# A Mamba block with a routed expert layer on one core: inputs laid out by partition, eps as a bias, ranking's bank copied by ACT, the first turn moved behind the last row product

## The chip, the cores and the metric

The kernel runs on one core of a Trainium2 chip. The metric is the device time of one execution in microseconds. The program is one launch; the inputs may be laid out anew on the host, but no arithmetic is done there. The engines are called as the profile calls them: PE is TensorE (its matmuls) and PEld its weight loads, DVE is VectorE, ACT is ScalarE, POOL is GpSimd, SP is the engine that only issues DMAs. Each of them works through its own queue in order.

## The reference

The input x has 4096 rows (tokens) of 256 numbers. Everything is fp32.

```python
# Mamba block, D_INNER 512, 16 states
xz = x @ W_in                                   # 256 -> 1024: conv half and gate half
y = causal depthwise conv(conv half, 4 taps) + conv_b
convolved = silu(y)
x_dbl = convolved @ W_x                         # 512 -> 33: delta, B, C
delta = softplus(x_dbl[..., :1])
h[t] = exp(delta * -exp(A_log)) * h[t-1] + delta * B * convolved[..., :16]
ssm = sum(h * C)                                # one number for each token
x = layernorm(x + ((ssm + convolved * D_param) * silu(gate half)) @ W_out)
# expert layer: each token goes to the one expert with the largest logit
expert = argmax(x @ Wr.T + br)                  # 8 experts
out = relu(x @ W1[expert].T + b1[expert]) @ W2[expert].T + b2[expert]
x = layernorm(x + out)                          # (x - mean) / sqrt(var + 1e-5)
```

## The kernel before, in words

**Two parts, overlapped.** The first part goes over the tokens in 8 blocks of 512 (NB = 8, TB = 512). The second part goes over 37 blocks of 128 rows that are sorted by expert (SURE = 37), and two more that run only if the data need them. PE's order is written out by hand: the scheduler is told to leave PE alone (line 109), and lines 808 to 915 are PE's program. The instructions of the other engines are put in order by the scheduler, by its own estimate of when each can run.

**Block k of the first part** is the body of the loop at line 808, and it works on several blocks of tokens at once. `project(k, 0..7)` (line 511) multiplies the block's transposed x (`xTb`) by W_in (`win`), 128 columns at a time: two matmuls of 512 columns (line 526). They are fp32, and the profile counts two records for each. The first four column blocks are evicted by ACT twice (lines 533 and 535), and DVE does the convolution's other three taps on them (line 539). The other four go through silu on ACT (line 531). For the very first product, `project(0, 0)`, the 512 tokens are split into two halves of 256.

For the block before (`a = k - 1`), `gauge` and `gauge_out` (lines 554 and 568) make delta, B and C; they contain the exponential `e` on ACT (line 590) and a chain of tiny DVE steps up to `sr` (line 611). `look` and `look_out` (lines 646 and 661) bring the router's share of x. `scan` (line 615) turns `sr` on PE into the bank `pt` (line 620) and runs the recurrence on DVE; its last step `hC` (line 631) is the last reader of `pt`. For the block before that (`b = k - 2`), `gate` (line 634) makes the product `py` and DVE's `cv`, and `project_out(b, 0..3)` (line 676) multiplies by W_out for 128 rows each (`po`, line 680), adds x and takes the statistics; after the fourth it takes the root (lines 693 to 696) and writes the normalised rows to `x1d` in HBM. `choose` (line 709) finds each row's expert. For `c = k - 3`, `rank` (line 735) counts each row's place within its expert with six small matmuls into one bank `pr`; DVE reads that bank (line 754, `rk`), works out `col` and `row` (line 761), compares them with constants into `colh` (DVE) and `rowh` (line 769: four instructions, on GpSimd for the blocks 0 to 4, on DVE for 5 to 7), and `place` (line 775) multiplies those two into the bank `pz` (line 780).

**PSUM.** The bank tag `tr` has two buffers that all the small products take in turn: `px`, `pxo`, `pr`, `pn`, `prx`, `pf`, `pt`, `pg`, `pz` and `pi`. A product therefore waits until the last but one has been read. When `blocks_of` takes a bank (`pn`, line 279) between `rank` and `look`, as in block 5 and block 7, `prx` (line 653) gets the bank of `pr`.

**The expert blocks** are a generator (`blocks`, line 481) whose quarters are drawn by `expert(n)`: two halves of the hidden layer (`hidden`, line 421: 16 matmuls of 128 columns in each, line 431), then the two halves of the second layer (`close`, line 445, line 452), with `turn(b + 1)` (line 411) ahead of the first of them. `turn` puts a block's gathered rows `xg` through PE into the bank `pg` and copies them (`xgT`). The gathers `xg` and the weights `we` are indirect DMAs from GpSimd (lines 399 and 405); they are issued in `prefetch`. `hidden` evicts its first half on ACT (line 439) and its second on DVE (line 441). `finish` ends with a layernorm of the block (line 238). The list `fill` (line 818) says how many quarters are drawn at each of the eight places of blocks 6 and 7 of the first part. The first turn, `turn(0)`, stands by itself in block 6, behind `scan` (line 862).

**The start.** SP and ACT issue the loads (lines 150 to 158): x's first block in four pieces of 128 KB, W_in in three pieces (the first 128 columns, 384 more, the other 512), and behind the pieces of x on ACT's queue the small `conv_w` and `conv_b`. The other small constants follow on SP's queue. PE does 12 transposes of the identity meanwhile (WARM, line 188).

Of the kernel before, what the change touches and what calls it, by code (L numbers as in the profile page):

```python
# [35 lines left out]
F32 = mybir.dt.float32  # L36
# [9 lines left out]
P = 128  # L46
# [16 lines left out]

WARM = 12

# [23 lines left out]
def mamba_moe(  # L89
# [4 lines left out]
    W_in: bass.AP,  # L94
    conv_w: bass.AP,
    conv_b: bass.AP,
    W_x: bass.AP,
    A_log: bass.AP,
    D_param: bass.AP,
    W_out: bass.AP,  # L100
    W_outT: bass.AP,
    WrT: bass.AP,
    br: bass.AP,
    experts: bass.AP,
# [21 lines left out]
    def load(i):  # L126

        xTb = a2.tile([P, DC, TB], F32, tag="xTb", name=f"xTb{i}")
        at = slice(i * TB, (i + 1) * TB)
        if i:  # L130
            nc.sync.dma_start(xTb, xT[:, at].rearrange("(c p) t -> p c t", p=P))

        xb = a2.tile([P, JT, D + NE], F32, tag="xb", name=f"xb{i}")
        st[i] = {"xTb": xTb, "xb": xb}
# [8 lines left out]

    win = const.tile([P, DC, 2 * DI], F32, name="win")
    first = TB // 2

    def columns(at):
        nc.sync.dma_start(win[:, :, at], W_in[:, at].rearrange("(c p) n -> p c n", p=P))

    for at in (slice(0, first), slice(first, TB)):  # L150
        nc.sync.dma_start(st[0]["xTb"][:, 0, at], xT[0:P, at])
        nc.scalar.dma_start(st[0]["xTb"][:, 1, at], xT[P : 2 * P, at])
        columns(slice(0, P) if at.start == 0 else slice(P, DI))
    cw = const.tile([P, CC, KC], F32, name="cw")
# [10 lines left out]
    al = const.tile([NS, 1], F32, name="al")  # L165
    dp = const.tile([P, CC], F32, name="dp")

    wout = const.tile([P, CC, D + NE], F32, name="wout")
    brb = const.tile([P, NE], F32, name="brb")
    nega = const.tile([NS, 1], F32, name="nega")  # L170

    def load_later():

        nc.sync.dma_start(wx[:, :, 0:XW], W_x.rearrange("(c p) n -> p c n", p=P))
        nc.sync.dma_start(al, A_log)
        nc.sync.dma_start(dp, D_param)
        nc.sync.dma_start(woutT, W_outT.rearrange("(c p) n -> p c n", p=P))
        nc.sync.dma_start(wout[:, :, 0:D], W_out.rearrange("(c p) d -> p c d", p=P))
        nc.sync.dma_start(brb, br.to_broadcast([P, NE]))
# [58 lines left out]
    def layernorm(pool, rows, n, done, name):  # L238
# [272 lines left out]
    def project(i, c):  # L511
# [11 lines left out]

        for at in (slice(0, first), slice(first, TB)) if i == c == 0 else (slice(0, TB),):
            for dc in range(DC):
                nc.tensor.matmul(  # L526
                    pm[:, at], lhsT=win[:, dc, c * P : (c + 1) * P], rhs=xTb[:, dc, at],
                    start=(dc == 0), stop=(dc == DC - 1),
                )
# [116 lines left out]
    def look(i):  # L646
# [3 lines left out]
        for dc in range(DC):  # L650
            for h in range(2):
                g = (2 * dc + h) * Q
                nc.tensor.matmul(
                    prx[g : g + Q, 0:n], lhsT=wr[:, dc, :],
                    rhs=st[i]["xTb"][:, dc, h * n : (h + 1) * n], start=True, stop=True,
                    tile_position=(0, g),
                )
# [18 lines left out]
    def project_out(i, j):  # L676
# [58 lines left out]
    def rank(i):  # L735
# [17 lines left out]
        rk = a2.tile([P, JT, NE], F32, tag="rk", name=f"rk{i}")  # L753
        nc.vector.tensor_tensor(rk, prv.rearrange("p (j e) -> p j e", e=NE), oh, ALU.mult)
        nc.vector.tensor_reduce(best, rk, AX.X, ALU.add)
# [52 lines left out]
    for k in range(NB):  # L808
# [169 lines left out]
```

## Time and profile before

| | us |
|---|---|
| median of 3 runs | 506.21 (505.69 to 506.3) |
| the profiled execution | 507.57 |
| its span in the profile | 505.9 |
| PE busy in the span | 492.2 |
| DVE busy in the span | 344.0 |
| first product of block 0 starts (line 526) | 4.59 |
| its second half starts | 6.21 |
| second column block starts | 7.85 |
| block 6 of the first part, first turn starts (line 415) | 176.63 |
| last matmul ends | 499.28 |

The span is the time from the first to the last instruction of the profiled execution; the time of the runs holds what lies around it as well. In the page, a group of instructions is given by its line, engine and operation, with what it writes and reads (out<-in). "Idle before" is the time in which the engine had nothing to do ahead of that instruction, with the instruction that released it. A matmul's end is modelled, so PE counts as busy also where it runs slower than it could. Names that end in a number are given without it. Stretches of time are counted from the start of the span.

### The profile page before, as it was taken

Reading aid. Unit: us, or ns where it says so; the run is one execution under the profiler, and the core shown is the slowest. Engines: PE = TensorE matmul, PEld = TensorE weight load, DVE = VectorE, ACT = ScalarE, POOL = GpSimd, SP = SyncE. Lnnn points to the kernel's source line nnn. Section 1 sums busy time; section 2 is a strip of 40 time slices with the busy share of each in tenths; the row PEclk is TensorE's granted clock in tenths of the full one; section 3 lists DMA queues with packets and bytes.
Section 4 is the critical chain, followed back from the end, with each engine's and each line's share of the span. In section 5 each row is a group of like instructions: output and inputs, shape, how many; then the busy total and the mean of one; then the engine's idle time right before and its main releaser. Section 6 shows DMA issues by size and latency. Waiting matters only on the chain.

```text
span 505.9 us, 7858 instructions
## 1 busy us (share of the span) xinstructions
PE 492.2 (97%) x2746; PEld 375.4 (74%) x2746; DVE 344.0 (68%) x1090; ACT 223.5 (44%) x472; POOL 181.7 (36%) x189
## 2 busy tenths in 40 slices
PE   7999999999999999999999999999999999999994
PEld 4443545555454576777889999999999999999994
DVE  2587869798999978869799785454545454545443
ACT  3786768778777865844351312212221222122111
POOL 2003011434355444324425234334433443344333
PEclk9998999999999999999999999999999999999998
DMA  7401012120309826407657598999755422811640
GB/s 234 147 1 43 0 43 83 43 84 24 102 1 378 318 63 220 188 0 268 231 198 261 210 361 303 344 349 349 284 202 195 159 105 53 344 58 32 229 182 23
DMA packets 23737, 84.87 MB, mean 168 GB/s; under 512 B 5934, under 2 KB 15665, under 8 KB 20242
## 3 DMA queue, kind: packets, MB, share of 16 engines
q0 software_dynamic: 9360, 69.60, 37.6%
q1 hardware_dynamic: 13378, 14.50, 9.0%
q8 instruction: 22, 0.36, 0.3%
q10 hardware_dynamic: 960, 0.27, 0.3%
q14 instruction: 17, 0.14, 0.1%
HBM read 102.75 MB, written 9.31 MB: 222 GB/s over the span
## 4 chain that ended last, share of the span: by engine, by line
PE 77%; DVE 15%; DMA 3%; ACT 2%; issue 2%; SPq 0%; POOLq 0%; POOL 0%; DVEq 0%; ACTq 0%
PE ph L431 26%; PE pe L452 25%; PE pm L526 11%; PE po L680 8%; DVE acc L539 7%; PE py L638 2%; DVE cv L640 2%; PE pg L415 2%; PE px L561 2%; DMA xg<-x1d,tidx 1%; DMA win<-in_W_in 1%; DVE lg L725 1%; PE pz L780 1%; PE pt L620 1%; DVE h L626 0%
## 5 line engine op out<-in xcount | busy, mean ns | idle before, releaser
L431 PEld LDWEIGHTS ph<-xgT,we 128*128 128x128 f32 x1184 | 138.5, 192 | 4.6 <-issue 1.6
L431 PE MATMUL ph<-xgT,we 128*128 128x128 f32 x1184 | 139.9, 275 | 0.0
L452 PE MATMUL pe<-we,hT 128*128 128x256 f32 x592 | 135.0, 380 | 0.0
L526 PE MATMUL pm<-xTb,win 128*128 128x512 f32 (+1 forms) x260 | 121.6, 598 | 1.2 <-DMA win<-in_W_in 0.7
L452 PEld LDWEIGHTS pe<-we,hT 128*128 128x128 f32 x592 | 109.4, 190 | 14.0 <-DVE best L724 0.8
L539 DVE SCALAR_TENSOR_TENSOR acc<-xc,cw,acc 128x512 f32<-128x512 f32 x96 | 76.0, 813 | 17.9 <-ACT acc L535 17.0
L247 ACT ACTIVATE sdm<-sdm 128x1 f32<-128x1 f32 x37 | 7.5, 203 | 173.9 <-DVE sdm L246 167.7
L526 PEld LDWEIGHTS pm<-xTb,win 128*128 128x128 f32 x260 | 47.2, 190 | 50.0 <-issue 43.3
L405 POOL DMA_INDIRECT we<-in_experts,widx x39 | 40.9, 1049 | 115.3 <-DVE r L467 82.5
L441 DVE TENSOR_SCALAR hT<-ph,we 128x128 f32<-128x128 f32 x148 | 42.6, 343 | 39.6 <-PE ph L431 35.6
L680 PE MATMUL po<-wout,sg 128*128 128x264 f32 x256 | 63.6, 391 | 0.0
L680 PEld LDWEIGHTS po<-wout,sg 128*128 128x128 f32 x256 | 46.3, 190 | 9.3 <-issue 2.9
L399 POOL DMA_INDIRECT xg<-x1d,tidx x39 | 38.1, 978 | 41.4 <-DVE xs L465 10.3
L467 DVE TENSOR_TENSOR r<-pe,xs 128x256 f32<-128x256 f32 x37 | 15.6, 423 | 53.8 <-PE pe L452 53.8
L473 POOL DMA_INDIRECT out<-y,tidx x37 | 38.0, 1028 | 38.5 <-DVE y L250 27.6
L644 POOL TENSOR_TENSOR sg<-cv,sg 128x512 f32<-128x512 f32 x22 | 31.1, 1428 | 54.0 <-DVE cv L640 39.7
L439 ACT ACTIVATE hT<-ph,we 128x128 f32<-128x128 f32 x148 | 42.1, 367 | 17.7 <-PE ph L431 9.5
L769 POOL TENSOR_SCALAR rowh<-lrow,row,code 128x256 f16<-128x256 bf16 x20 | 25.8, 1298 | 25.1 <-DVE row L761 17.3
L533 ACT COPY xc<-pm 128x512 f32<-128x512 f32 x32 | 18.6, 581 | 20.0 <-PE pm L526 19.9
L640 DVE SCALAR_TENSOR_TENSOR cv<-cv,dp,py 128x512 f32<-128x512 f32 x32 | 23.4, 735 | 5.7 <-PE py L638 5.6
L531 ACT ACTIVATE sg<-pm 128x512 f32<-128x512 f32 x32 | 19.0, 594 | 14.9 <-PE pm L526 12.2
L535 ACT ACTIVATE acc<-pm,cb,cw 128x512 f32<-128x512 f32 x32 | 25.1, 783 | 0.0
(156 smaller groups left out, 474.4 us busy)
## 6 DMA issues: line engine op xcount, KB each, us to landing
xb<-in_x SPq DMA_DIRECT2D x8, 512.0 KB, 7.6
x1d<-x SPq DMA_DIRECT2D x8, 512.0 KB, 5.4
xTb<-in_xT SPq DMA_DIRECT2D x7, 512.0 KB, 3.4
we<-in_experts,widx POOLq DMA_INDIRECT x39
xg<-x1d,tidx POOLq DMA_INDIRECT x39
out<-y,tidx POOLq DMA_INDIRECT x37
win<-in_W_in SPq DMA_DIRECT2D x1, 512.0 KB
we<-in_W_outT SPq DMA_DIRECT2D x1, 512.0 KB
```

The lines of the kernel that those rows point to most:

```text
L399: nc.gpsimd.indirect_dma_start(out=xgs[n], out_offset=None, in_=x1d[0 : index[n][0], :], in_offset=bass.IndirectOffsetOnAxis(ap=index[n][1 ...
L405: nc.gpsimd.indirect_dma_start(out=wes[n][:, :], out_offset=None, in_=experts, in_offset=bass.IndirectOffsetOnAxis(ap=weights[n], axis=0), ...
L431: nc.tensor.matmul(ph[:, n * P : (n + 1) * P], lhsT=we[:, at : at + P], rhs=xgT[:, dc * P : (dc + 1) * P], start=(dc == 0), stop=(dc == DC ...
L439: nc.scalar.activation(hT[:, fc, :], ph[:, n * P : (n + 1) * P], AF.Relu, bias=bias)
L441: last[b] = nc.vector.tensor_scalar(hT[:, fc, :], ph[:, n * P : (n + 1) * P], bias, 0.0, ALU.add, ALU.max)
L452: nc.tensor.matmul(py[:, 0:D], lhsT=hT[:, fc, :], rhs=we[:, at : at + D], start=(fc == 0), stop=(fc == FC - 1),)
L473: moved = nc.gpsimd.indirect_dma_start(out=out, out_offset=bass.IndirectOffsetOnAxis(ap=index[b][1], axis=0), in_=ys[b][:, 0, :], in_offse ...
L526: nc.tensor.matmul(pm[:, at], lhsT=win[:, dc, c * P : (c + 1) * P], rhs=xTb[:, dc, at], start=(dc == 0), stop=(dc == DC - 1),)
L539: nc.vector.scalar_tensor_tensor(acc, xc[:, c, k : k + TB], cw[:, c, k : k + 1], acc, ALU.mult, ALU.add)
L640: nc.vector.scalar_tensor_tensor(cv[:, c, :], cv[:, c, :], dp[:, c : c + 1], py, ALU.mult, ALU.add)
L644: eng.tensor_tensor(sg[:, c, :], cv[:, c, :], sg[:, c, :], ALU.mult)
L680: nc.tensor.matmul(po[:, 0 : D + NE], lhsT=sg[:, c, j * P : (j + 1) * P], rhs=wout[:, c, :], start=(c == 0), stop=(c == CC - 1),)
```

## The change

Five edits are made together.

1. Inputs are laid out on the host so that each partition reads one contiguous piece. `xT` becomes 8 blocks of [128 partitions, 2 halves of tokens, 2 chunks, 256 tokens], `W_in` becomes [128 partitions, 8 column blocks, 2 chunks, 128 columns]. At the start, x's first block comes in two pieces of 256 KB (one on SP's queue, one on ACT's), and W_in's first block stands ahead of x's second half on ACT's queue. `conv_w`, `conv_b`, `D_param`, `Wr`, `br` and `A_log` become one array `small` of 49 numbers for each partition, in one DMA on ACT's queue. The router's weights are copied from there into `wr` by DVE.
2. In both layernorms, eps is no longer added by DVE: it is the bias of ACT's square root, from a constant that GpSimd sets at the start.
3. In `rank`, ACT copies the bank `pr` to `rk`, and DVE multiplies that in place.
4. `turn(0)` stands behind `project_out(b, 3)` and `choose(b)` in place of ahead of them, and the first two quarters of expert block 0 move from the seventh place of block 6 to the eighth, where all four are now drawn: behind `project(6, 7)` and `place(3)`.
5. Nine warm-up transposes instead of twelve.

```diff
-WARM = 12
+WARM = 9
...
-        xTb = a2.tile([P, DC, TB], F32, tag="xTb", name=f"xTb{i}")
-        at = slice(i * TB, (i + 1) * TB)
+        xTb = a2.tile([P, 2, DC, TB // 2], F32, tag="xTb", name=f"xTb{i}")
         if i:
-            nc.sync.dma_start(xTb, xT[:, at].rearrange("(c p) t -> p c t", p=P))
+            nc.sync.dma_start(xTb, xT[i])
...
-    win = const.tile([P, DC, 2 * DI], F32, name="win")
-    first = TB // 2
-
-    def columns(at):
-        nc.sync.dma_start(win[:, :, at], W_in[:, at].rearrange("(c p) n -> p c n", p=P))
-
-    for at in (slice(0, first), slice(first, TB)):
-        nc.sync.dma_start(st[0]["xTb"][:, 0, at], xT[0:P, at])
-        nc.scalar.dma_start(st[0]["xTb"][:, 1, at], xT[P : 2 * P, at])
-        columns(slice(0, P) if at.start == 0 else slice(P, DI))
-    cw = const.tile([P, CC, KC], F32, name="cw")
-    nc.scalar.dma_start(cw, conv_w.rearrange("(c p) k -> p c k", p=P))
-    cb = const.tile([P, CC], F32, name="cb")
-    nc.scalar.dma_start(cb, conv_b)
-    columns(slice(DI, 2 * DI))
+    win = const.tile([P, 2 * CC, DC, P], F32, name="win")
+    nc.sync.dma_start(st[0]["xTb"][:, 0], xT[0, :, 0])
+    nc.scalar.dma_start(win[:, 0], W_in[:, 0])
+    nc.scalar.dma_start(st[0]["xTb"][:, 1], xT[0, :, 1])
+    nc.sync.dma_start(win[:, 1:CC], W_in[:, 1:CC])
+    small_ones = const.tile([P, small.shape[1]], F32, name="small")
+    nc.scalar.dma_start(small_ones, small)
+    nc.sync.dma_start(win[:, CC:], W_in[:, CC:])
...
     wr = const.tile([P, DC, Q], F32, name="wr")
     nc.vector.memset(wr, 0.0)
-    nc.sync.dma_start(wr[:, :, 0:NE], WrT.rearrange("(c p) e -> p c e", p=P))
+    nc.vector.tensor_copy(wr[:, :, 0:NE], wrs.rearrange("p (c e) -> p c e", e=NE))
...
+    eps = const.tile([P, 1], F32, name="eps")
+    nc.gpsimd.memset(eps, EPS)
...
-        nc.vector.tensor_scalar(sd, mv[:, :, 1], EPS, None, ALU.add)
-        nc.scalar.activation(sd, sd, AF.Sqrt)
+        nc.scalar.activation(sd, mv[:, :, 1], AF.Sqrt, bias=eps)
...
-        nc.vector.tensor_tensor(rk, prv.rearrange("p (j e) -> p j e", e=NE), oh, ALU.mult)
+        nc.scalar.copy(rk, prv.rearrange("p (j e) -> p j e", e=NE))
+        nc.vector.tensor_tensor(rk, rk, oh, ALU.mult)
...
-        fill = {NB - 2: (0, 0, 0, 0, 0, 0, 2, 2), NB - 1: (1, 1, 2, 1, 1, 1, 1, 1)}.get(k, (0,) * 8)
+        fill = {NB - 2: (0, 0, 0, 0, 0, 0, 0, 4), NB - 1: (1, 1, 2, 1, 1, 1, 1, 1)}.get(k, (0,) * 8)
...
-        if k == NB - 2:
-
-            turn(0)
         if have(b):
             project_out(b, 3)
             choose(b)
         expert(fill[6])
+        if k == NB - 2:
+
+            turn(0)
         project(k, 7)
         if have(c):
             place(c)
```

The square root's two lines are changed in the same way in `layernorm` and in `project_out`; the matmuls that read `xTb` and `win` are adapted to the new layout. In the program as built, PE's instructions differ only in the number of warm-up transposes and in the order of block 6; ACT's eight new copies stand in its queue behind the exponential `e` for the first three ranks.

More of the change, by code (lines that the diff above doesn't have):

```diff
@@ L94, in mamba_moe @@
     W_in: bass.AP,
-    conv_w: bass.AP,
-    conv_b: bass.AP,
     W_x: bass.AP,
-    A_log: bass.AP,
-    D_param: bass.AP,
     W_out: bass.AP,
     W_outT: bass.AP,
-    WrT: bass.AP,
-    br: bass.AP,
+    small: bass.AP,
     experts: bass.AP,
@@ L141, in mamba_moe @@
     load(0)
-    win = const.tile([P, DC, 2 * DI], F32, name="win")
-    first = TB // 2
-    def columns(at):
-        nc.sync.dma_start(win[:, :, at], W_in[:, at].rearrange("(c p) n -> p c n", p=P))
-    for at in (slice(0, first), slice(first, TB)):
-        nc.sync.dma_start(st[0]["xTb"][:, 0, at], xT[0:P, at])
-        nc.scalar.dma_start(st[0]["xTb"][:, 1, at], xT[P : 2 * P, at])
-        columns(slice(0, P) if at.start == 0 else slice(P, DI))
-    cw = const.tile([P, CC, KC], F32, name="cw")
-    nc.scalar.dma_start(cw, conv_w.rearrange("(c p) k -> p c k", p=P))
-    cb = const.tile([P, CC], F32, name="cb")
-    nc.scalar.dma_start(cb, conv_b)
-    columns(slice(DI, 2 * DI))
+    win = const.tile([P, 2 * CC, DC, P], F32, name="win")
[6 more added lines that the diff above has]
+    nc.sync.dma_start(win[:, CC:], W_in[:, CC:])
+    parts, at = [], 0
+    for n in (CC * KC, CC, CC, DC * NE, NE, 1):
+        parts.append(small_ones[:, at : at + n])
+        at += n
+    cw, cb, dp, wrs, brb, al = parts
+    cw = cw.rearrange("p (c k) -> p c k", k=KC)
+    al = al[0:NS]
     wr = const.tile([P, DC, Q], F32, name="wr")
     nc.vector.memset(wr, 0.0)
-    nc.sync.dma_start(wr[:, :, 0:NE], WrT.rearrange("(c p) e -> p c e", p=P))
+    nc.vector.tensor_copy(wr[:, :, 0:NE], wrs.rearrange("p (c e) -> p c e", e=NE))
     wx = const.tile([P, CC, H], F32, name="wx")
     nc.vector.memset(wx, 0.0)
-    al = const.tile([NS, 1], F32, name="al")
-    dp = const.tile([P, CC], F32, name="dp")
     wout = const.tile([P, CC, D + NE], F32, name="wout")
-    brb = const.tile([P, NE], F32, name="brb")
     nega = const.tile([NS, 1], F32, name="nega")
@@ L174, in load_later @@
         nc.sync.dma_start(wx[:, :, 0:XW], W_x.rearrange("(c p) n -> p c n", p=P))
-        nc.sync.dma_start(al, A_log)
-        nc.sync.dma_start(dp, D_param)
         nc.sync.dma_start(woutT, W_outT.rearrange("(c p) n -> p c n", p=P))
         nc.sync.dma_start(wout[:, :, 0:D], W_out.rearrange("(c p) d -> p c d", p=P))
-        nc.sync.dma_start(brb, br.to_broadcast([P, NE]))
         nc.sync.dma_start(x1d[T : T + 1, :], lists[0:1, 0:D])
@@ L522, in project @@
         pm = bank("mm", f"pm{i}_{c}")
-        for at in (slice(0, first), slice(first, TB)) if i == c == 0 else (slice(0, TB),):
+        for at in (slice(0, 1), slice(1, 2)) if i == c == 0 else (slice(0, 2),):
             for dc in range(DC):
                 nc.tensor.matmul(
-                    pm[:, at], lhsT=win[:, dc, c * P : (c + 1) * P], rhs=xTb[:, dc, at],
-                    start=(dc == 0), stop=(dc == DC - 1),
+                    pm.rearrange("p (h t) -> p h t", h=2)[:, at], lhsT=win[:, c, dc, :],
+                    rhs=xTb[:, at, dc, :], start=(dc == 0), stop=(dc == DC - 1),
                 )
@@ L654, in look @@
                     prx[g : g + Q, 0:n], lhsT=wr[:, dc, :],
-                    rhs=st[i]["xTb"][:, dc, h * n : (h + 1) * n], start=True, stop=True,
+                    rhs=st[i]["xTb"][:, h, dc, :], start=True, stop=True,
                     tile_position=(0, g),
@@ L693, in project_out @@
         sd = s_["sd"] = a2.tile([P, JT], F32, tag="sda", name=f"sda{i}")
-        nc.vector.tensor_scalar(sd, mv[:, :, 1], EPS, None, ALU.add)
-        nc.scalar.activation(sd, sd, AF.Sqrt)
+        nc.scalar.activation(sd, mv[:, :, 1], AF.Sqrt, bias=eps)
         nc.vector.reciprocal(sd, sd)
@@ L950 @@
     b2 = np.broadcast_to(given("L0_ffn_b2")[:, None, :], (NE, P, D)).reshape(NE * P, D)
+    small = [
+        given("L0_attn_conv_w").reshape(CC, P, KC).transpose(1, 0, 2).reshape(P, CC * KC),
+        given("L0_attn_conv_b").reshape(CC, P).T,
+        given("L0_attn_D_param").reshape(CC, P).T,
+        given("L0_ffn_Wr").reshape(NE, DC, P).transpose(2, 1, 0).reshape(P, DC * NE),
+        np.broadcast_to(given("L0_ffn_br").reshape(1, NE), (P, NE)),
+        np.resize(given("L0_attn_A_log"), (P, 1)),
+    ]
     arrays = {
         "x": x,
-        "xT": x.T,
-        "W_in": given("L0_attn_W_in"),
-        "conv_w": given("L0_attn_conv_w").reshape(DI, KC),
-        "conv_b": given("L0_attn_conv_b").reshape(CC, P).T,
+        "xT": x.reshape(NB, 2, TB // 2, DC, P).transpose(0, 4, 1, 3, 2),
+        "W_in": given("L0_attn_W_in").reshape(DC, P, 2 * CC, P).transpose(1, 2, 0, 3),
         "W_x": given("L0_attn_W_x"),
-        "A_log": given("L0_attn_A_log").reshape(NS, 1),
-        "D_param": given("L0_attn_D_param").reshape(CC, P).T,
         "W_out": given("L0_attn_W_out"),
         "W_outT": given("L0_attn_W_out").T,
-        "WrT": given("L0_ffn_Wr").T,
-        "br": given("L0_ffn_br").reshape(1, NE),
+        "small": np.concatenate(small, axis=1),
         "experts": np.concatenate([w1, w2, b1, b2], axis=1),
```

## The prediction

> **What bounds the kernel now.** I read the page first, then TensorE's waits, busy time by stage, the chain that ended last, and the timelines of three places: the start, block 5 and block 6 of the projection.
>
> The page and two stages (columns: stretch, then busy us and instructions of PE, PEld, DVE, ACT, POOL, granted clock, DMA share, GB/s):
>
> ```profile
> PE 492.2 (97%) x2746; PEld 375.4 (74%) x2746; DVE 344.0 (68%) x1090; ACT 223.5 (44%) x472; POOL 181.7 (36%) x189
> ...
> 124.00:152.00 28.00, 27.19 (x113) 14.73 (x112) 26.73 (x88) 21.68 (x36) 11.23 (x9) 1.00 0.19 58
> ...
> 185.00:300.00 115.00, 114.74 (x686) 92.69 (x685) 94.85 (x348) 52.41 (x110) 43.02 (x38) 1.00 0.58 207
> 300.00:495.00 195.00, 195.00 (x1353) 183.85 (x1352) 97.02 (x334) 36.17 (x136) 78.86 (x79) 1.00 0.59 214
> ```
>
> From 185 us on TensorE is idle 0.26 us in 310: whatever delay TensorE has at 185 us reaches the end whole, and a lighter VectorE buys nothing there. In blocks 2 to 5 the chain alternates: about 20 us of VectorE without a gap, then some 7 us of TensorE. So only the start, the joints of blocks 2 to 6, and the tail can move the time.
>
> TensorE's waits (columns: total us, times, longest):
>
> ```profile
> PE pg L415 <- DMA xg<-x1d,tidx: 1.0, 1, 1.0
> ...
> PE prx L653 <- DVE rk L754: 0.8, 1, 0.8
> PE pm L526 <- DMA win<-in_W_in: 0.7, 2, 0.5
> ...
> PE pm L526 <- DMA xTb<-in_xT: 0.5, 1, 0.5
> ```
>
> The change aims at exactly these. The places themselves, from the timelines (start us, duration, engine, line; in brackets the idle time before):
>
> ```profile
> 7.85 0.70 PE L526 MATMUL pm<-xTb,win 128*128 128x512 f32 x1 [0.51 <-DMA win<-in_W_in]
> ...
> 143.12 0.17 DVE L754 TENSOR_TENSOR rk<-pr,oh 128x32 f32<-128x32 f32 x1
> ...
> 143.34 0.64 PE L653 MATMUL prx<-xTb,wr 128*32 128x256 f32 x8 [0.81 <-DVE rk L754]
> ...
> 143.49 0.21 ACT L590 ACTIVATE e<-e 128x4 f32<-128x4 f32 x1
> 143.71 1.28 ACT L531 ACT_TABLE_LOAD   x1
> ...
> 175.02 0.60 PE L620 MATMUL pt<-ident,sr 128*80 128x128 f32 x4
> 176.63 0.41 PE L415 MATMUL pg<-ident,xg 128*128 128x128 f32 x2 [1.01 <-DMA xg<-x1d,tidx]
> ...
> 175.73 5.12 POOL L769 TENSOR_SCALAR rowh<-lrow,row,code 128x256 f16<-128x256 bf16 x4 [1.15 <-PE pt L620]
> 181.60 0.69 DVE L631 TENSOR_TENSOR hC<-pt,h 16x512 f32<-16x512 f32 x1
> 183.99 0.61 PE L780 MATMUL pz<-colh,rowh 128*128 128x128 f16 x8
> ```
>
> See in the last three that `pz` (line 780) started 3.1 us after GpSimd's `rowh` was done (180.85) and 1.7 us after `hC` (182.29) had freed its PSUM bank. That slack was covered by 3.6 us of expert matmuls (line 431).
>
> [...] while the 16-byte pieces of `conv_w` were moving, the rate was 136 GB/s from 4 to 5 us and 235 from 5 to 6, against 267 to 336 in the microseconds around. [...] so ACT's new copy needs no table load; the existing copies of line 672 (194 ns) come without one. [...] Here the clock was 0.50 from 45.5 to 48.8 us, after TensorE had little but tiny matmuls from 42.3 to 44.7; it is needed for a rival below.
>
> **The start.** TensorE runs without a break from 7.85 us (second column block of W_in) to 24.7, and the chain follows it from there, so an earlier 7.85 is worth itself. Both kernels need the same 1024 KB before that matmul: x 512, W_in 512. What goes is small pieces (1 KB and 512 B rows become 2, 1 and 3 KB) and the 512 pieces of `conv_w` in the middle of them. The dip costs (320-136)+(320-235) = 269 KB, or 0.84 us at the 320 GB/s around it. Larger rows at some 330 instead of 285 GB/s between 2 and 4 us give 90 KB, 0.3 us. Sum 1.1; I take 1.2, since W_in's rest is also issued near 1.25 instead of 2.25 us. Bounds: -0.3 (x's second half now stands behind a W_in block on ACT's queue and shares bandwidth with 384 KB; its two matmuls, 1.1 us, come before the 7.85) and 2.0 (the first matmul needs 384 KB in both kernels and had them at 4.59; a tenth to a fifth more rate over the 2.6 us since the first byte at 2.0 makes that 4.0 to 4.3, and both halves back to back, 1.10 and 1.13 us, 6.2 at the latest; with PE's gap-free pace of 0.43 per pair of records, 5.8). The `small` transfer (25 KB) lands before the first eviction ends, as conv_w did (1.7 + 5.8 = 7.5 against 7.85); the DVE copy into `wr` is one tiny instruction ahead of an idle VectorE (7.3 us idle there). Three warm-up transposes fewer (0.235 each) only lengthen a wait for data. **-1.2.**
>
> **eps as bias.** 45 VectorE instructions of 0.15 us go (lines 246 and 694). In the blocks line 694 stands in VectorE's 1.0 us wait for `py`, and the square root behind it starts at the end of its table load (98.46, against 98.39 for the sum), so nothing. In the 37 expert blocks TensorE is the bound: nothing. In the tail the last block's sum stands on the path, 500.45 to the root at 500.63: **-0.2.** The memset of `eps` on GpSimd delays the identity by under 0.1 us, at a time when TensorE waits for data.
>
> **ACT copies ranking's bank.** VectorE's `rk` loses its PSUM read (0.17 us either way), ACT gets a 0.19 us copy. What counts is the place: in the built order ACT's copy of ranks 0 to 2 stands behind `e` (line 590), which itself stands behind a table load. In block 5 `e` ends at 143.70, so the copy frees the bank at 143.90 and `prx` starts at 143.95 instead of 143.34: the wait of 0.8 that it should remove becomes 1.4. Behind `prx` stand projection, `pt`, `pz`, `py`, all without slack up to VectorE's start at 155.18: **+0.6.** In blocks 3 and 4 `prx` has another bank; there `rk` now waits for the copy some 0.05 us on VectorE's gapless stretch: **+0.1** for both. On ACT the 0.19 us pushes a table load and evictions that TensorE awaits 1 us later.
>
> **The turn moved.** Its two matmuls and the xgT copy move; no DMA moves (the gathers are issued earlier, GpSimd's order is the same). Before, from 175.62 (end of `pt`): 1.01 wait, `pg` 0.25, `po` 1.78, experts 3.6, `pm` 1.72, `pz` 0.45. After: `po` fills the wait (-1.0), then `pg`, then `pm` to 179.4, and then **`pz` with nothing in between**. It needs `hC`, which VectorE reaches at about 180.9 + 0.65 = 181.6 (same work as before, one or two short steps moved), and `rowh`. `rowh` even starts later: in the new order VectorE does `po_1`'s addition and statistics (0.43 + 0.43) ahead of `rk`, so `row` ends at 176.3 instead of 175.5, and GpSimd's four instructions (5.12) at 181.7. So TensorE stands from 179.4 to 181.7, finishes `pz` at 182.1, the experts at 185.7; before, it was there at 184.4. **+1.3**, and 0.15 more because ACT puts the four x1 steps (2.07 us) between the hidden block's second and third eviction. Total **+1.45**; bounds -1.0 (no wait) and +1.7.
>
> **Sum** on the profiled execution (507.57; span 505.9 and 1.67 around it): -1.2 - 0.2 + 0.6 + 0.1 + 1.45 = +0.75, so 508.3. It stands 1.36 above the median of the runs, 506.21; the same difference on that gives **506.9**. A measurement of this kernel tells some 0.2% (1.0 us) from no change.
>
> **Rivals.**
> - *Slower: the clock.* TensorE stands 2.2 us at `pz`, followed by 0.45 us of narrow matmuls. [...] the clock is halved for 3.4 us and 1.7 us of dense expert work are lost: 506.9 + 1.7 = 508.6. For it: the drop at 45.5 followed 2.4 us of little work. Against: idle of 1.4 us at 175.6 brought none. [...]
> - *Faster: the turn gains.* Spans on GpSimd are rough, and `rowh` and `hC` might be ready at 179.4: -1.2 - 0.2 + 0.7 - 1.0 = -1.7, 504.5. Against: two independent engines would both have to be 2 us early.
> - *The copy does what it says.* If ACT gets to it before 142.5, block 5's wait goes: -0.8 instead of +0.6: 505.5. Against: `e` stands before it on an in-order engine.
>
> **Chances.** Forecast 0.42, clock 0.30, turn 0.17, copy 0.11. Within 0.2% (505.2 to 507.2) fall most of the forecast's share (0.36), most of the copy's (0.07) and a little of the others (0.04): 0.47. Slower: the clock's 0.28 and 0.05 of the forecast's: 0.33. Faster: 0.20. The forecast's own range is 505.9 to 507.7 (the start's bounds nearly whole); with the clock and part of the turn, 505.0 to 508.8.
>
> **What would show it.** Right: line 526 with 512 columns starts at 6.3 to 7.0; `prx` in block 5 waits about 1.4 us for ACT; no wait of `pg` for xg; `pz` in block 6 waits about 2.2 us for GpSimd or VectorE; from there TensorE busy to the end. Wrong: `pz` without a wait, a `prx` wait below 0.8, or a start later than 7.5. A stretch at clock 0.50 near 182 us is the first rival.

## The result and the profile after

The changed kernel takes **510.26 us** in the median of 6 runs (509.85 to 512.31); the kernel before, with the runs beside it, 506.25 (505.69 to 508.15, 6 runs). The ratio is 1.0074 with a 95% interval of 1.0054 to 1.0094: 4.0 us slower, above the upper end of the forecast (508.8). The profiled execution of the changed kernel took 510.02 (span 508.1).

One thing has to be known to read these numbers: in some executions of nearly every version TensorE's clock is halved for 3.41 us once or twice (a drop), which costs some 1.6 us each time, and a run's mean granted clock tells it (0.996 to 0.998 for none, 0.993 to 0.995 for one, 0.990 to 0.991 for two). The profile before has a drop, from 45.46 to 48.87 us; the profile after has none. "Undropped" below means runs without one: for the changed kernel 5 of 6, median 510.03; for the kernel before 506.1 to 506.3 in every comparison where it had more than ten runs.

Line numbers after are smaller by 10 or 11: 526 is 515 (`pm`), 653 is 642 (`prx`), 780 is 769 (`pz`), 431 is 420 (`ph`); the ranking copy is 742. The page and the stages shown before:

```profile
PE 492.5 (97%) x2743; PEld 376.1 (74%) x2743; DVE 337.2 (66%) x1046; ACT 227.5 (45%) x479; POOL 184.0 (36%) x190
...
124.00:152.00 28.00, 26.71 (x107) 14.47 (x106) 26.21 (x87) 21.38 (x36) 11.12 (x9) 1.00 0.17 58
185.00:300.00 115.00, 114.69 (x686) 92.32 (x684) 91.57 (x329) 52.00 (x114) 42.56 (x37) 1.00 0.56 201
300.00:495.00 195.00, 195.00 (x1351) 183.76 (x1350) 93.66 (x311) 38.59 (x135) 78.97 (x79) 1.00 0.60 218
```

VectorE lost 6.8 us of work and ACT gained 4; TensorE has as much as before and is still busy without a gap from 185 us on. So the loss lies ahead of 185 us, in waits or in matmuls that run slowly (these count as busy). TensorE's waits:

```profile
PE pz L769 <- DVE xgT L408: 2.2, 1, 2.2
PE idle L179 <- POOL ident masks.py:199: 1.6, 1, 1.6
PE pm L515 <- DMA xTb<-in_xT: 1.4, 1, 1.4
PE prx L642 <- ACT rk L742: 1.3, 1, 1.3
```

The wait of `pg` for its gathered rows (1.0) is gone. In its place `pz` waits 2.2; `prx` waits 1.3 and not 0.8; the first matmul 1.4.

**Where the 4 us come in.** The same instruction in both timelines: `pw`, a small product behind the third column block, starts at 13.38 us instead of 11.38, and `py` of the first block at 45.70 instead of 43.70: **+2.0, all of it from the start**.

```profile
11.38 0.51 PE L368 MATMUL pw<-wr,ones 128*128 128x8 f32 x4
...
13.38 0.51 PE L357 MATMUL pw<-wr,ones 128*128 128x8 f32 x4
```

The first of these lines is from before, the second from after. Then the profile before loses 1.64 to its own halved clock, so from here on I count differences of the difference: blocks 2 to 4 give back 0.23, block 5 costs 0.44, block 6 from `pt` to the sixth `py` (189.93 before, 192.24 after) 1.80, the rest gives 0.1 to 0.2 back. Sum 2.0 - 0.23 + 0.44 + 1.80 - 0.15 = 3.9, against 4.0 between the medians.

**The start.** TensorE's weight loads, after and then before (start, duration, engine, line, instructions; in brackets the idle time before):

```profile
5.19 1.36 PEld L515 LDWEIGHTS pm<-xTb,win 128*128 128x128 f32 x4 [1.77 <-DMA win<-in_W_in]
7.35 2.21 PEld L515 LDWEIGHTS pm<-xTb,win 128*128 128x128 f32 x6 [0.80 <-DMA xTb<-in_xT]
10.08 0.34 PEld L515 LDWEIGHTS pm<-xTb,win 128*128 128x128 f32 x1 [0.52 <-issue]
...
11.24 0.19 PEld L515 LDWEIGHTS pm<-xTb,win 128*128 128x128 f32 x1 [0.24 <-issue]
```

```profile
4.56 0.73 PEld L526 LDWEIGHTS pm<-xTb,win 128*128 128x128 f32 x4 [0.54 <-issue]
6.20 0.73 PEld L526 LDWEIGHTS pm<-xTb,win 128*128 128x128 f32 x4 [0.91 <-DMA xTb<-in_xT]
```

Two things differ. The first half of x can be used 0.6 us later and the second 1.15 us later. And the same four loads take 1.36 us instead of 0.73; one load takes 0.34 at 10.08 and 0.19 from then on. That is TensorE at half its clock up to about 10.5 us. The column of the granted clock says 1.00 all the while, because it has no records there: the trace's first record begins at 10.68 us after, at 4.50 before. I read that first record as the moment from which full clock was granted.

**The rates.** Busy time by stretch of 1 us, before and then after (last column GB/s, the one before it the DMA engines' share):

```profile
2.00:3.00 1.00, 1.00 (x7) 1.00 (x6) 0.00 (x0) 0.25 (x1) 1.00 (x9) 1.00 0.92 267
3.00:4.00 1.00, 1.00 (x6) 1.00 (x5) 0.00 (x0) 1.00 (x1) 0.85 (x7) 1.00 1.07 300
```

```profile
2.00:3.00 1.00, 1.00 (x7) 1.00 (x6) 0.00 (x0) 0.82 (x1) 1.00 (x8) 1.00 0.50 131
3.00:4.00 1.00, 0.82 (x4) 0.42 (x2) 0.00 (x0) 0.46 (x1) 0.89 (x7) 1.00 0.81 184
```

The larger rows came at a half to three fifths of the rate, with the DMA engines at shares of 0.50 and 0.81, in the two microseconds on which the start depends.

**Blocks 5 and 6**, from the timeline after:

```profile
142.33 1.28 ACT L579 ACT_TABLE_LOAD   x1
...
143.62 0.21 ACT L579 ACTIVATE e<-e 128x4 f32<-128x4 f32 x1
143.73 0.17 ACT L742 COPY rk<-pr 128x32 f32<-128x32 f32 x1
...
143.95 0.64 PE L642 MATMUL prx<-xTb,wr 128*32 128x256 f32 x8 [1.29 <-ACT rk L742]
...
175.97 1.95 PE L669 MATMUL po<-wout,sg 128*128 128x264 f32 x8
...
177.11 5.35 POOL L758 TENSOR_SCALAR rowh<-lrow,row,code 128x256 f16<-128x256 bf16 x4 [1.95 <-DVE row L750]
...
177.75 0.38 PE L404 MATMUL pg<-ident,xg 128*128 128x128 f32 x2
177.97 1.88 PE L515 MATMUL pm<-xTb,win 128*128 128x512 f32 x4
...
181.54 0.42 DVE L408 COPY xgT<-pg 128x256 f32<-128x256 f32 x1
...
182.00 0.69 DVE L620 TENSOR_TENSOR hC<-pt,h 16x512 f32<-16x512 f32 x1
182.02 0.33 PE L769 MATMUL pz<-colh,rowh 128*128 128x128 f16 x3 [2.17 <-DVE xgT L408]
...
182.52 0.45 PE L769 MATMUL pz<-colh,rowh 128*128 128x128 f16 x5 [0.18 <-POOL rowh L758]
...
182.81 3.79 PE L420 MATMUL ph<-xgT,we 128*128 128x128 f32 x32
```

These are the forecast's pictures: the copy behind `e`, itself behind a table load; `pz` with nothing between it and `pm`, waiting for VectorE and then for GpSimd's `rowh`. On VectorE it waited for the turn's own copy `xgT`, which ended at 181.96, and not for `hC`, which the forecast named: `hC` was still running until 182.69 when `pz` had started.

### The profile page after: what moved, and what is told of

Read it like the earlier page. It is cut to its first block, busy times and chain, and to the rows that moved or that the text cites. A ratio compares the mean times of both kernels' runs of the same rounds, so it can differ in the third digit from the quotient of the medians.

```text
span 508.1 us, 7822 instructions
## 1 busy us (share of the span) xinstructions
PE 492.5 (97%) x2743; PEld 376.1 (74%) x2743; DVE 337.2 (66%) x1046; ACT 227.5 (45%) x479; POOL 184.0 (36%) x190
## 4 chain that ended last, share of the span: by engine, by line
PE 61%; issue 1%; POOL 1%; ACT 1%; POOLq 0%; DVE 0%
PE ph L420 26%; PE pe L441 24%; PE po L669 4%; PE pm L515 3%; PE pg L404 2%; PE px L550 1%; PE py L627 1%; POOL rowh L758 1%; PE pz L769 0%; ACT x L689 0%; POOLq L967 0%; POOL out L462 0%; PE pxo L563 0%; PE pi L331 0%; PE pt L609 0%
## 5 line engine op out<-in xcount | busy, mean ns | idle before, releaser
L236 ACT ACTIVATE sdm<-mvm,eps 128x1 f32<-128x1 f32 x37 | 10.9, 295 | 169.4 <-DVE mvm L234 167.5
L515 PEld LDWEIGHTS pm<-xTb,win 128*128 128x128 f32 x260 | 48.6, 196 | 50.8 <-issue 43.0
L528 DVE SCALAR_TENSOR_TENSOR acc<-xc,small,acc 128x512 f32<-128x512 f32 x96 | 75.7, 811 | 12.8 <-ACT acc L524 11.9
L633 POOL TENSOR_TENSOR sg<-cv,sg 128x512 f32<-128x512 f32 x22 | 32.5, 1493 | 51.4 <-DVE cv L629 39.5
L629 DVE SCALAR_TENSOR_TENSOR cv<-cv,small,py 128x512 f32<-128x512 f32 x32 | 23.3, 737 | 5.2 <-PE py L627 5.1
L524 ACT ACTIVATE acc<-pm,small 128x512 f32<-128x512 f32 x32 | 25.1, 783 | 0.0
```

The costliest lines, as they stand in the source:

```text
L515: nc.tensor.matmul(pm.rearrange("p (h t) -> p h t", h=2)[:, at], lhsT=win[:, c, dc, :], rhs=xTb[:, at, dc, :], start=(dc == 0), stop=(dc = ...
L528: nc.vector.scalar_tensor_tensor(acc, xc[:, c, k : k + TB], cw[:, c, k : k + 1], acc, ALU.mult, ALU.add)
L633: eng.tensor_tensor(sg[:, c, :], cv[:, c, :], sg[:, c, :], ALU.mult)
```

## The experiments

The theory after this reading: the start costs 2.0 us, through the new layout (slow first rows) and through TensorE's low clock; the turn costs 1.5 to 1.8, the copy 0.4, eps nothing. Rivals: the late data alone (no clock); the order of the pieces on the two queues, not the layout; and, for block 6, GpSimd's later rows, whatever the turn's place.

All numbers of the start in one table. `pw` is the first matmul behind the third column block; "full clock" is where the trace's records of it begin; the rate is that from 2 to 3 and from 3 to 4 us. The last columns are medians of all runs and of the undropped ones (their number of all).

| run | transposes | GB/s | full clock from | `pw` at | all | undropped |
|---|---|---|---|---|---|---|
| before | 12 | 267, 300 | 4.50 | 11.38 | 506.25 | |
| after | 9 | 131, 184 | 10.68 | 13.38 | 510.26 | 510.03 (5 of 6) |
| warm_12 | 12 | 116, 164 | 9.26 | 12.62 | 511.77 | 510.26 (2 of 6) |
| warm_16 | 16 | 134, 179 | 7.61 | 11.88 | 510.78 | 508.41 (1 of 6) |
| turn_back | 9 | 131, 181 | 10.41 | 13.25 | 508.82 | 508.64 (4 of 7) |
| rank_direct | 9 | 121, 163 | 9.99 | 13.09 | 511.43 | 509.62 (2 of 6) |
| split_16 | 16 | 309, 255 | 6.66 | 11.71 | 509.87 | none of 6 |
| dense_16 | 16 | 218, 372 | 5.04 | 10.24 | 509.60 | none of 7 |
| start_only | 9 | 129, 183 | 11.52 | 13.69 | 508.06 | 507.95 (15 of 19) |
| warm_9_before | 9 | 272, 279 | 7.79 | 11.35 | 507.85 | 507.72 (12 of 22) |
| x_dense_16 | 16 | 67, 282 | 7.76 | 11.58 | 509.60 | none of 6 |
| w_dense_16 | 16 | 201, 387 | 4.72 | 10.09 | 508.81 | none of 6 |
| dense_back | 20 | 266, 369 | 6.01 | 11.15 | 505.83 | 505.83 (22 of 22) |
| dense_early | 24 matmuls | 244, 376 | 5.45 | 13.79 | 508.74 | 508.46 (9 of 12) |
| pad_16 | 16 | 114, 304 | 4.45 | 11.18 | 509.09 | 507.51 (4 of 18) |
| dense_9 | 9 | 230, 382 | 8.02 | 11.31 | 510.90 | none of 6 |
| dense_back_16 | 16 | 270, 373 | 6.70 | 11.06 | 505.35 | 505.24 (16 of 22) |

The rates and full clock are of one profiled execution each. Where full clock begins is in part chance: in the four profiles with nine transposes and the change's layout it lies at 9.99, 10.41, 10.68 and 11.52 us. The rates repeat better: in all six profiles whose start has the change's layout and order they are 116 to 134 and 163 to 184. The kernel before had medians of 506.65, 507.44, 507.64 and 507.59 beside these runs, since more of its executions there had a drop; its undropped medians were 506.31, 506.07, 506.29 and 506.28.

**warm_12 and warm_16: more transposes, nothing else.**

```
-WARM = 9
+WARM = 12        (warm_16: 16)
```

> The changed kernel with twelve warm-up transposes instead of nine, nothing else. Theory 1 (TensorE's clock is low at the start because it had done too little before the first data came): the eight 256-wide matmuls of block 0 come every 0.21 to 0.24 us and not every 0.43 us; the second half then takes 1.1 us instead of 2.1 and the second column block starts at about 8.5 instead of 9.4 us; with 0.5 us more in that block, 508.9 (1.4 less than the changed kernel's 510.3). Theory 2 (only the data come later, the pace follows them): the pace stays at 0.43 us and the time at 510.3. If three transposes (0.7 us more) are too few to hold the clock over the wait for data, theory 1 would see no change here but one with sixteen.

> The changed kernel with sixteen warm-up transposes: TensorE then works until about 5.4 us, up to the landing of the first half of x (5.2 us). Theory 1 (clock): full pace from the first real matmul, the second half starts when x's second half lands (7.35 us), the second column block at about 8.5 us, 508.8 in all. Theory 2 (data only): 0.2 us later at the first matmul, nothing at the second half, 510.3.

Three more transposes did not shorten the undropped runs (510.26, two runs, against 510.03). Full clock came 1.4 us sooner in the profile and `pw` 0.76, but that is about as much as the four profiles with nine differ among themselves. Seven more did: `pw` 1.5 us sooner, 508.41 in the one undropped run. In the loads of warm_16 the first four are still at half pace, the next six at full pace:

```profile
5.05 1.35 PEld L515 LDWEIGHTS pm<-xTb,win 128*128 128x128 f32 x4
7.37 1.26 PEld L515 LDWEIGHTS pm<-xTb,win 128*128 128x128 f32 x6 [0.97 <-DMA xTb<-in_xT]
```

Among the runs with the layout of the change, `pw` follows the time of full clock: from 7.61 to 11.52 it moves from 11.88 to 13.69, 0.46 us for each us. Loads of 0.34 us where full pace has 0.19 would give 0.44, and the theory of late data alone has no place for it.

**turn_back: the turn where it was.**

```
-... NB - 2: (0, 0, 0, 0, 0, 0, 0, 4) ...
+... NB - 2: (0, 0, 0, 0, 0, 0, 2, 2) ...
...
         scan(a)
+    if k == NB - 2:
+        turn(0)
     if have(b):
...
-    if k == NB - 2:
-        turn(0)
     project(k, 7)
```

> The changed kernel with the first turn and the expert steps around it put back where they were. Theory (the moved turn takes the cover from before pz and costs 1.5 to 1.8 us there): 508.6, with pz after 3.6 us of expert matmuls and no wait, and the wait of pg for its gathered rows back at 1.0 us. Rival (the step in block 6 comes from GpSimd's later rows, whatever the turn's place): pz still waits 1 us or more, 510 or above.

508.82 in all, undropped 508.64: 1.4 less than the changed kernel (1.9 between the two profiled executions). From its timeline:

```profile
176.26 0.41 PE L404 MATMUL pg<-ident,xg 128*128 128x128 f32 x2 [0.27 <-ACT rparts L661]
176.50 1.95 PE L669 MATMUL po<-wout,sg 128*128 128x264 f32 x8
178.84 3.84 PE L420 MATMUL ph<-xgT,we 128*128 128x128 f32 x32 [0.39 <-DVE xgT L408]
182.51 1.88 PE L515 MATMUL pm<-xTb,win 128*128 128x512 f32 x4
184.23 0.61 PE L769 MATMUL pz<-colh,rowh 128*128 128x128 f16 x8
```

`pz` comes without a wait behind 3.8 us of expert matmuls. The rival is out. The wait of `pg` was 0.3 here and not 1.0.

**rank_direct: VectorE reads the bank itself.**

```
-nc.scalar.copy(rk, prv...)
-nc.vector.tensor_tensor(rk, rk, oh, ALU.mult)
+nc.vector.tensor_tensor(rk, prv..., oh, ALU.mult)
```

> The changed kernel with VectorE reading the ranking bank itself again, ACT's copy gone. Theory (the copy stands behind a table load on ACT and lets prx of block 5 start 0.6 us late, 0.44 of which reach VectorE's scan): the wait of prx back from 1.3 to 0.8 us, 509.8. Rival (the delay is gone again before block 6, where TensorE waits 2.2 us for GpSimd anyway): the wait of prx shrinks but the time stays at 510.3 within 0.2.

The wait of `prx` is back at 0.8, and the two undropped runs are 509.53 and 509.70, 0.4 less. Two runs are few, but the trace says the same: from the fourth `py` to the fifth are 27.69 us here, 28.11 in the changed kernel and in turn_back, 27.67 in the kernel before. The median of all six, 511.43, is above the changed kernel's only because four of them had one drop or two.

**split_16: the old order of the pieces, the new layout, sixteen transposes.** (`xTb0` stands for block 0's `xTb`, `at` for the columns.)

```
+for h in range(2):
+    nc.sync.dma_start(xTb0[:, h, 0], xT[0, :, h, 0])
+    nc.scalar.dma_start(xTb0[:, h, 1], xT[0, :, h, 1])
+    nc.sync.dma_start(win[:, at], W_in[:, at])      # block 0, then 1 to 3
```

> The changed kernel with sixteen warm-up transposes and its new layouts, but the first pieces handed to the queues as in the kernel before: of each half of x, one chunk on SP's queue and one on ACT's, then the W_in block on SP (ACT no longer carries W_in and then x's second half). Compared with the run with sixteen transposes (508.4 where the clock never fell after the start), so that the clock is out of it. Theory A (the order: x's second half stands behind a W_in block on ACT's queue while SP's larger rows take the bandwidth): the second half lands near 6.2 and not 7.3 us, the second column block starts at about 7.9 and not 8.5 us, 507.5. Theory B (the layout itself moves slowly at first): the rate from 2 to 4 us stays at 130 to 180 GB/s against 270 to 300 before, and the time at 508.4.

The rate from 2 to 4 us is high, 309 and 255, but then it falls to 108 and 161 from 4 to 6 us, when W_in's rows are under way. `pw` at 11.71 is 0.17 before warm_16's, with full clock 1 us sooner. So the order only moves the slow stretch: mostly theory B. All six runs had one drop (509.36 to 510.05), so the totals cannot be set against 508.41.

**dense_16: each first piece dense in memory, sixteen transposes.** (The two arrays; the transfers are adapted.)

```
-"xT": ...transpose(0, 4, 1, 3, 2)      "W_in": ...transpose(1, 2, 0, 3)
+"xT": ...transpose(0, 1, 4, 3, 2)      "W_in": ...transpose(2, 1, 0, 3)
```

> The changed kernel with sixteen warm-up transposes, its order and row sizes kept, but each first piece dense in memory: a half of x is 256 KB in a row (rows of 2 KB, 2 KB apart, not 4), a W_in block 128 KB in a row (rows of 1 KB, 1 KB apart, not 8). Theory B (rows at a stride of 4 and 8 KB are slow at first): the rate from 2 to 4 us rises from 130 and 180 to 270 GB/s or more, the first matmul could start at 4.4, the second half at 6.2, 507.5. Theory A (order): all as with sixteen transposes, 508.4.

```profile
2.00:3.00 1.00, 1.00 (x7) 1.00 (x6) 0.00 (x0) 0.82 (x1) 1.00 (x8) 1.00 0.97 218
3.00:4.00 1.00, 1.00 (x6) 1.00 (x5) 0.00 (x0) 0.46 (x1) 0.89 (x7) 1.00 1.06 372
```

No data are awaited any more, `pw` starts at 10.24: 1.64 us before warm_16's and 1.14 before the kernel before. The order of the pieces and the sizes of the first three are warm_16's, so it is the layout. Every run had a drop here too, so 509.60 hides it.

**start_only: the kernel before with the new start alone.** (Diff: of the change, only the transfers, layouts and `WARM = 9`.)

> The kernel before with the new layouts, transfers and nine transposes only; eps, ranking's bank and the turn as before. If the parts add up, the start alone makes 1.9 to 2.0 us of the changed kernel's loss: 508.2 against 506.3 where the clock never falls after the start. Rival (the parts act on one another: later starts elsewhere absorb some): 507.3 or below.

Undropped 507.95 against 506.07: +1.9, as the parts' sum wants. `pw` is at 13.69.

**warm_9_before: the kernel before with nine transposes.**

> The kernel before with nine instead of twelve warm-up transposes and nothing else. If the clock of TensorE at the start is what the three transposes bought, full clock is granted later than 4.5 us, the first halves of column block 0 take up to 2 us each, and the time is 0.8 to 1.3 us above 506.3. If the transposes only fill a wait, 506.3 within 0.2, with full clock from about 4.5 us.

Half a miss. None of its 12 undropped runs is below 507.27, while 16 of the kernel before's 20 beside them are at 506.51 or less; the medians are 1.65 us apart. But the profiled execution does not show it: full clock came at 7.79 and not 4.50, yet `pw` stands at 11.35, because the slow matmuls only fill the wait for the second column block's data, which the kernel before awaits until 7.84 anyway. Full clock later than that in other executions would explain the runs; no profile of one shows it, so this stays argued.

The kernel before has such runs as well: of its undropped runs beside these experiments, 21 of 74 lie between 507.4 and 507.9 and the others at 506.8 or less. Nine transposes put all undropped runs into this upper group or near it.

So layout and transposes, the two parts of the start, do not add up. Nine transposes with the old layout cost 1.65 us, nine with the new one 1.9 (start_only), and the changed kernel is no faster with twelve than with nine (warm_12, two undropped runs). By these runs either part alone makes most of the loss.

**x_dense_16 and w_dense_16: only x dense, only W_in dense.** (Diff: one of dense_16's two lines each.)

> As the run with dense pieces and sixteen transposes, but only x is dense (rows of 2 KB, 2 KB apart); W_in's blocks keep the change's layout (rows of 1 and 3 KB, 8 KB apart). The dense run moved 218 and 372 GB/s from 2 to 3 and 3 to 4 us, the changed kernel 131 and 184. If x's 4 KB stride is the slow one: the dense run's rates, second column block at about 7 us. If W_in's 8 KB stride is: 130 to 180 GB/s, as in the changed kernel, second column block at 8 us or later.

> As the run with dense pieces and sixteen transposes, but only W_in's blocks are dense (rows of 1 KB; the rest of W_in in 1 KB pieces too); x keeps the change's layout (rows of 2 KB, 4 KB apart). If W_in's 8 KB stride is the slow one: the dense run's rates (218 and 372 GB/s), second column block at about 7 us. If x's 4 KB stride is: 130 to 180 GB/s, second column block at 8 us or later.

Only x, then only W_in:

```profile
2.00:3.00 1.00, 1.00 (x7) 1.00 (x6) 0.00 (x0) 0.82 (x1) 1.00 (x8) 1.00 0.41 67
3.00:4.00 1.00, 1.00 (x6) 1.00 (x5) 0.00 (x0) 0.47 (x1) 0.89 (x7) 1.00 0.90 282
```

```profile
2.00:3.00 1.00, 1.00 (x7) 1.00 (x6) 0.00 (x0) 0.82 (x1) 1.00 (x8) 1.00 0.75 201
3.00:4.00 1.00, 1.00 (x6) 1.00 (x5) 0.00 (x0) 0.47 (x1) 0.89 (x7) 1.00 1.03 387
```

In those two microseconds warm_16 moved 313 KB (134 + 179), x_dense 349, w_dense 588, dense_16 590. W_in's layout is nearly all of it. The runs with one drop agree: their medians are 509.57 with only x dense (5 runs) and 508.81 with only W_in dense (6).

**pad_16: W_in's rows 9 KB apart, not 8.**

```
+"W_in": np.pad(..., ((0, 0), (0, 1), (0, 0), (0, 0)))      # a ninth, unused block
```

> As the changed kernel with sixteen transposes, but W_in is stored with one unused block of 1 KB behind the eight of each partition, so that its rows lie 9 KB apart and not 8; the pieces moved are the same. If the stride of 8 KB is slow in itself (a power of two), the rate from 2 to 4 us rises to that of the dense W_in (201 and 387 GB/s) and the second column block starts at about 7 us. If scattered rows of W_in are slow at any stride, 130 and 180 GB/s stay, with the second column block at 8 us or later.

Between the two: 114 and 304, 418 KB. The second microsecond comes most of the way to the 387 of dense W_in, the first does not gain. So the stride of 8 KB is part of it (105 of the 275 KB that dense W_in gained) and scattered rows are the rest. Distance alone is no rule: in the kernel before, x's first rows of 1 KB lie 16 KB apart and W_in's rows of 512 B 4 KB apart, and these came at 267 and 300. Why the first microsecond of W_in's scattered rows is slow stays open; so does whether the pieces of 1 KB, into which the dense layout also cuts the rest of W_in, help.

Its 18 runs give the price of the drops: 507.51 without (4 runs), 509.11 with one (12), 511.16 with two (2). One of them is at the standing of `pz`; stages, then TensorE, of its profile:

```profile
179.00:182.00 3.00, 0.68 (x4) 0.15 (x2) 2.94 (x6) 2.24 (x4) 2.96 (x3) 0.99 0.00 0
182.00:185.30 3.30, 3.28 (x18) 3.29 (x19) 1.90 (x10) 0.00 (x0) 0.00 (x0) 0.50 0.00 0
```

```profile
182.02 0.71 PE L769 MATMUL pz<-colh,rowh 128*128 128x128 f16 x5 [0.18 <-POOL rowh L758]
182.52 5.15 PE L420 MATMUL ph<-xgT,we 128*128 128x128 f32 x32
```

TensorE works 0.68 of 3 us, and its clock is 0.50 for the 3.3 after; 32 expert matmuls take 5.15 us, 3.79 in the profile of the changed kernel. This is the forecast's first rival, at its place, behind the stand that it named (2.16 us here).

**dense_9: dense pieces, nine transposes.** (Diff: dense_16's, with `WARM = 9`.)

> The changed kernel with dense first pieces and its nine transposes. With the data fast, the first matmul could start at 4.5 us. If the clock has its own share, full clock is granted only at 7 us or later, the second column block starts 1 us or more later than with sixteen transposes (6.8 us) although no data are awaited, and the runs without a later drop of the clock lie about 1 us above theirs. If the low clock was only a consequence of the long wait for data, full clock by 5.5 us and a start as good as with sixteen.

The first matmul comes at 4.18 us, nothing is awaited after it, and still `pw` is at 11.31 instead of 10.24: full clock came at 8.02. The clock's own share in the start is 1.07 us between these two profiles. The undropped runs that I wanted to compare did not occur; with one drop there are two, 508.47 and 509.09, no slower than dense_16's (509.39), so the times alone do not show it.

**dense_back and dense_back_16: what the experiments point to.** Dense pieces, the turn and the ranking as before, eps as bias; twenty and sixteen transposes.

> What the experiments point to: dense first pieces, twenty warm-up transposes, the turn and ranking's bank as in the kernel before, eps as bias. Start 1.1 us earlier than the kernel before (its second group of weights, pw, at 10.3 us, not 11.4), the turn at nothing, eps 0.1 to 0.2: 504.8 where the clock never falls after the start (before: 506.0), and 1.2 us below the kernel before in the median. Rival (the earlier start is lost again at the joints of blocks 2 to 5): 505.7 or above, pw early but the sixth py no earlier.

> As the kernel with dense pieces, twenty transposes and the rest as before (505.83), with sixteen transposes: the first matmul comes at 5.1 and not 6.0 us. Where full clock is granted by 5 us, 0.9 us less (504.9); where it comes at 7 us or later, the same or 0.5 us more. Median 505.2 if the first is the usual case, 505.9 or above if not.

505.83, ratio to the kernel before 0.9974 (0.9965 to 0.9983), and 505.35, ratio 0.9976 (0.9964 to 0.9988): **both below both kernels**. With twenty no run of 22 had a drop, with sixteen 6 of 22. The first misses the number of the start (`pw` at 11.15, I had 10.3) and so the time (505.83, I had 504.8): twenty transposes hold up the first matmul until 5.96 us. With sixteen it comes at 5.11, as expected, but full clock came only at 6.70 in the profile and `pw` at 11.06. The undropped gain is 0.5 and 1.0 us, and none of these undropped runs lies in the upper group of the kernel before. The new start is not so much sooner as steadier: where the old one gets full clock early, as in eps_before's profile (5.38 us), `pw` stands at 11.24. More of the difference of medians comes from the drops avoided.

**dense_early: the warm-up on a tile of ones, earlier.** (Diff: `transpose(idle, ident, ident)` becomes `matmul(idle, lhsT=ones, rhs=ones)`, with `ones` written by VectorE.)

> As the last, but the warm-up is 24 matmuls on a tile of ones that VectorE writes first (so TensorE works from about 1.2 and not 1.65 us)[...]. If the clock at the start still costs something in the last kernel's runs, full clock is granted no later than 5 us and the median falls by 0.3 to 0.6 us more; if not, the same within 0.2.

A mis-sized experiment: 24 matmuls of this kind are 48 instructions and held TensorE to 8.6 us, so the start came 2.6 us late (`pw` 13.79) and the time rose by as much. Of the question it says only that full clock came at 5.45.

**eps_before: eps alone.**

> The kernel before with eps as the bias of the square root and nothing else. The forecast's step: one VectorE instruction of 0.17 us less on the path of the tail, nothing elsewhere: 0.2 us less than the kernel before, which the timing can hardly tell from none; in the trace, the last block's root follows its statistics without a sum between. Rival (the root now waits for ACT to read the statistics itself, or the identity comes later behind the new memset): the same or up to 0.2 us more, with the first transpose at 1.64 and not 1.61 us.

Ratio 1.0001 (0.9989 to 1.0013); undropped 506.12 against 506.28. From its timeline:

```profile
498.52 0.18 DVE L246 BATCH_NORM_AGGREGATE mvm<-stm 128x2 f32<-128x6 f32 x1
498.74 0.29 ACT L248 ACTIVATE sdm<-mvm,eps 128x1 f32<-128x1 f32 x1 [5.26 <-DVE mvm L246]
499.07 0.16 DVE L249 RECIPROCAL sdm<-sdm 128x1 f32<-128x1 f32 x1 [0.36 <-ACT sdm L248]
```

Before, from the statistics (500.23) to the reciprocal (500.87) were 0.64 us; here 0.55. The root got 0.09 longer (0.29 for 0.20), which eats half of the sum that went.

## Why the prediction was wrong, step by step

**The start: the step that failed.** The forecast had -1.2 with bounds of -2.0 and +0.3; the trace has +2.0. The second column block starts at 9.22 us (7.85 before), past the 7.5 that the forecast named as a sign of being wrong. Three sentences of it were wrong.

- *"Larger rows at some 330 instead of 285 GB/s between 2 and 4 us"*. Measured: 131 and 184, from rows of 1 to 3 KB. I priced a transfer by the size of its rows and never asked how they lie in memory; the change put W_in's rows 8 KB apart, and dense rows of the same first pieces came at 218 and 372 (dense_16). 1 KB of padding behind W_in's 8 KB raised the second microsecond (304 for warm_16's 179), not the first (114 for 134); in the kernel before, x's first rows lay 16 KB apart and came, with W_in's, at 267 and 300.
- *"The dip costs [...] 269 KB"*. I put the dip from 4 to 6 us down to `conv_w`'s 16-byte pieces. split_16 has no `conv_w` and has such a dip, 108 and 161, with W_in's rows under way, and dense_16 has none. So the dip does not need `conv_w`, and taking it out did not bring the 0.84 us; what part it had in the kernel before, no run isolates.
- *"Three warm-up transposes fewer [...] only lengthen a wait for data."* They cost the clock. Before, twelve transposes are 2.82 us of work from 1.61 us on, and the records of full clock begin at 4.50; after, nine are 2.18 us, TensorE then waits 1.40 us for x, and they begin at 10.68. With nine for twelve and nothing else full clock came at 7.79 (warm_9_before). With dense pieces it came at 8.02 behind nine and at 5.04 behind sixteen, and `pw` 1.07 us later (dense_9); the seven transposes of warm_16 brought `pw` back by 1.5. How much work it takes, and when, was not shown: behind the same nine transposes and layout it came anywhere from 9.99 to 11.52.

**eps**: -0.2 forecast, 0.09 less in the tail, nothing in the times.

**The copy**: right in its mechanism. `prx` waits for the copy behind `e`, and block 5 costs 0.44 for the 0.6 forecast; taking the copy out gave 0.4. That `prx` starts at 143.95, the very number forecast, is luck: the block had begun 0.13 us late. The 0.1 for blocks 3 and 4 is not to be seen: they gave back 0.23 of the late start.

**The turn**: the cover lost ahead of `pz` was right, and the size near. `pz` waits 2.2 and then 0.2, for VectorE and then GpSimd, as written. But the step on VectorE was another: the forecast had `pz` wait for `hC` and did not count the moved copy `xgT` as a wait, and the trace has it start 0.06 us behind `xgT`, with `hC` just begun. That `xgT` ended at 181.96, near the 181.6 that the forecast had for `hC`, is luck; `rowh` came at 182.46 for the 181.7 forecast. The way from `pt` to the second `pg` grew from 9.42 to 10.91 us (+1.49; forecast 1.3), and from there to the sixth `py` from 5.49 to 5.80 (+0.31; forecast 0.15), 1.80 in all, just above the bound of 1.7. turn_back took 1.4 to 1.9 off.

**The rivals.** The clock at `pz` was given 0.30. It is real: eight of the ten profiles of versions with the moved turn show the clock at 0.50 for 3.41 us between 178.8 and 187.5, and none of the other eight profiles does. But in the changed kernel's own 6 runs only one had a drop, so it is not the cause of the 4.0 us; with the start 3.2 us off, the forecast's other terms give 506.9 + 3.2 = 510.1 without it. These terms (eps, copy, turn) sum to 1.95 forecast and 1.86 measured, in part because their errors cancel. The idle of 1.4 us at 175.6 that the forecast set against this rival is 1.01 in the line that it shows. "The turn gains" and "the copy does what it says" are out.

## What to carry to other kernels

A transfer is priced by how its rows lie in memory as well as by their size: lay a piece that something waits for densely (218 and 372 GB/s here, against 134 and 179 for the same sizes in the change's layout), and look at the rate in the microseconds in which it moves. Before taking away work that seems to do nothing on TensorE, look at when full clock comes without it (at 8.02 us behind nine transposes, at 5.04 behind sixteen, with dense pieces), and look at the clock behind a new wait (0.50 for 3.41 us in eight of ten profiles with the wait of some 2 us at `pz`). Work between two dependent steps is a cover: moving it to fill a wait of 1 us is paid by the wait that it covered, here 2.2 us.

## What the runs showed of the hardware that was not expected

- Behind nearly the same stand at `pz` the clock was halved or was not. In the changed kernel's own profile and in warm_16's it lasts 2.17 us, and the 32 expert matmuls behind it take 3.79 us; in those of warm_12, pad_16, dense_16 and rank_direct it lasts 2.16, 2.16, 2.17 and 2.03, and they take 5.06 to 5.42. What decides between the two was not shown. One drop costs 1.6 us (pad_16), a little under half of 3.41. The counts of dropped runs do not tell how often the stand brings one: drops near 45 us are among them, and the kernel before has one in about half of its runs (21 of 41 beside split_16).
- The granted clock's column shows 1.00 before its first record. At the start the pace of the weight loads (0.34 or 0.19 us each) is the surer sign.
- The drop at 45.46 in the profile before follows a stretch in which TensorE counts as mostly busy: 2.72 of the 3.18 us from 42.28 on, 2.07 of them in matmuls with 8 columns (`pwo`, 0.95) or 16 rows (`py`, 1.12). What part of this brought the drop was not shown.
